# Four of a pass's seven second-layer products in quarters, in another order, with sums in every home of first-layer weights

## The chip, the core and the metric

The kernel runs on one core of one Trainium2 chip. The metric is the device time of one execution, in microseconds (us), as the median of several runs. Beside the times there is one execution taken by the hardware profiler; its trace gives every instruction with its start, length, engine, and what ended a wait before it. Engines are named as the profile names them: PE is TensorE (matmuls; PEld its weight loads), DVE is VectorE, ACT is ScalarE, POOL is GpSimd, and SP issues DMAs (transfers). SBUF is the memory beside the engines, in which tiles live; PSUM is the memory that matmuls write.

## The reference

Everything is fp32. There are 8 sequences of 512 rows and 512 columns. The reference runs four layers over them; three fifths of the time go to the part that matters here, the feed-forward network of the second layer and the expert network of the third:

```python
h = _ln(x) * g2 + beta2                                # second layer, one set of weights
ff = _gelu2(h @ W1 + b1) @ W2 + b2
x = x + ff
...
h = gelu(input @ Wi[expert] + bi[expert])              # third layer, one expert for each sequence
o = h @ Wo[expert] + bo[expert]
r = o + input; y = norm(r) * gamma[expert] + beta[expert]
```

W1 and Wi are 512x2048, W2 and Wo 2048x512. The fourth layer makes two 32-column bases orthonormal (a Gram-Schmidt process, one column after the other), and adds to every row of y a low-rank response, scaled by a gate that needs the mean of all rows of the sequence.

## The kernel before

The last stage (`mlp_stage`) makes 16 passes, q = 0 to 15, one for each sequence and network: passes 0 to 7 are the second layer, 8 to 15 the experts. A pass multiplies twice. Its **first layer** works through the 2048 hidden columns in four groups g of 512. Its **second layer** takes all four groups together.

Both layers save multiplications by a scheme with seven products in place of eight (Strassen's, in Winograd's form): each operand is cut in 2x2 quadrants, here of 256 columns, called A00 to A11 on the left and B00 to B11 on the right. Seven products are made of quadrants and of sums of quadrants (S1 to S4 on the left, T1 to T4 on the right), and added up in the right combination:

- p1 = A00 B00, p2 = A01 B10, p3 = S4 B11, p4 = A11 T4, p5 = S1 T1, p6 = S2 T2, p7 = S3 T3.

In the second layer the left operand is the activations (`acts`, [128, 4 groups, 4, 512]), the right one the tile `wo` of the same shape. `second` (L1635) makes one such product with 128x256 matmuls, into a PSUM tile y_28, y_32 and so on, by the number of its first slot. `third` (L1694) makes a product by a second level of the same scheme, in quarters of 128 columns: 7 x 4 matmuls of 128x128, 28 in place of 16 twice as wide. It accumulates into two PSUM tiles (y_48a with four quarters, y_48b with three), and DVE adds these up in a tile `yw`. In an fp32 trace each matmul is two instructions.

Before the change p7 and p4 are in quarters. The order of the second layer is p1 (slots 28 to 31), p5 (32), p2 (36), p6 (40), p3 (44), p7 (48), p4 (52). In the last pass p4 is two half products, with the end of the kernel between (`last_row`).

**Slots and hooks.** A pass has 56 slots. Slots 0 to 27 are the 28 products of the first layer (four matmuls each, seven products for each group); slots from 28 on are fourths of a second-layer product. All other work is hung on slots: `at(hooks, s, f)` puts f before the matmuls of slot s. Compute instructions are pinned (`pin`), so each engine gets them in the order in which they are written and works through them in that order. A hook's slot decides only its place in each engine's queue; when it runs is decided by what it waits for.

**Sums.** The left sums of the second layer are DVE's work. ACT first copies one operand to PSUM (`stage`, two buffers), so that DVE reads one operand from PSUM and one from SBUF. The right sums are subtractions on POOL (`gadd`, L1220). `t13` makes T1 and T3, `t2s2` T2 and S2 after each group of p5, `t4s4` T4 and S4 after each group of p2. The quarter sums are made by `quarters`: three left steps (`of_left`) and four subtractions on POOL (`of_right`), for p7 at slots 28 to 31 (right) and 40 to 42 (left), for p4 at 41 to 44 (right) and 43, 45, 47 (left).

**Homes.** The first-layer weights of one group (`wi`, 1 MB) live in one of four SBUF buffers, x0 to x3, which I call homes. Once a pass's first layer is through, homes x1 to x3 hold the quarter sums of p7 and p4; x0 is free, and takes the next pass's first group by a load at slot 21 (L2054). x1 is loaded at slot 52, x2 and x3 at slot 0 of the next pass, then `wo` (4 MB). `w_quads` makes the S sums of a loaded group on POOL: group 0 at slot 46 of the pass before (L2077), group 1 at slot 1, group 2 at slot 7, group 3 at slot 14. The first layer's third product of a group is the first that reads S2.

**What else shares the engines.** In passes 0 to 7 a Gram-Schmidt step stands at four slots (11, 25, 44, 51; L2079): `gs_norm` lets DVE reduce a broadcast row `qb` and POOL take a root (`gs_d`), and two slots later `gs_b` updates `qm` on DVE and issues the next broadcast of `qb` by two DMAs on POOL (L1259). In those passes the next sequence is also normalised. In passes 9 to 15 the tail of the sequence before runs along: `tail_gamma`, `tail_feats` (PSUM tile pf), `gate` (pg), `strength` (pz), `add_beta` (a 128x2048 addition on POOL, L1918), and four tiles `po` from slot 45, which DVE adds to the rows at slots 47, 48, 49 and 51 (`tail_add`, L1930). At slot 51 `b_quads` makes the eight right sums of the next pass's first layer on DVE, with both operands in SBUF.

**PSUM.** Products, pf, pg, pz and po take turns in six buffers, in the order in which they are written: a tile waits until the reader of the sixth tile before it is done.

Of the kernel before, what the change touches and what calls it, by code (L numbers as in the profile page):

```python
# [20 lines left out]
NB = 8  # L21
S = 512
D = 512
# [1174 lines left out]
def mlp_stage(tc, a, small, xp, io, wo8, x1d, ident, eidx, sigs, layernorm, rstd_of, phalf, wl3, g2, b1, first):  # L1198
# [4 lines left out]
    with ExitStack() as ctx:  # L1203
# [348 lines left out]
        def run(q, hooks):  # L1552
# [21 lines left out]
            def s13(g):  # L1574
# [2 lines left out]
                add(ss[g], t, act_quad(g, 1, 1))  # L1577
                add(act_quad(g, 1, 0), act_quad(g, 0, 0), t, ALU.subtract)

            for g in range(NG):  # L1580
                out = {
                    (i, j): acts[:, g, 2 * i : 2 * i + 2, H * j : H * j + H]
# [46 lines left out]
                        add(out[0, 1], p[6], u2)  # L1629
                        gelu(0)  # L1630

            wo, ts = wos[q], {}
            tvs = extra["t", q]

            def second(s, A, B, each=None):  # L1635
                y = ps.tile([P, 2, H], F32, name=f"y_{q}_{s}", tag="u", bufs=6)
                for g in range(NG):
                    go(s + g)
                    if s == 28 and g == 1:
                        stage(f"s13_{NG - 1}", act_quad(NG - 1, 1, 0))  # L1640
                    if s == 28 and g == 2:
                        s13(NG - 1)
                    for i in range(2):
                        for m in range(2):
                            mm(
                                y[:, m, :], A(g)[:, i, m * P : (m + 1) * P], B(g)[:, i, :],
                                g + i + m == 0, g + i + m == NG + 1,
                            )
                    if each:
                        each(g)  # L1650
                return y

            def quarters(key, i, j, wi_, wj, homes):


                def left(k, m):
                    o = H * i + P * m
                    return acts[:, :, 2 * j + k, o : o + P]

                def right(k, n):  # L1660
                    o = H * wj + P * n
                    return wo[:, :, 2 * wi_ + k, o : o + P]

                s1, s2, s4, t1, t2, t4 = homes
                L, M = left, right
                four[key] = dict(
                    a=((L(0, 0), M(0, 0)), (s2, t2), (L(0, 1), M(0, 1)), (s1, t1)),
                    b=((L(1, 0), M(1, 0)), (s4, M(1, 1)), (L(1, 1), t4)),
                )
                sub = ALU.subtract  # L1670
                of_left = [
                    lambda: (stage(key + "a", L(0, 1)), stage(key + "b", L(0, 0))),
                    lambda: (
                        add(s1, st[key + "a"], L(1, 1)),
                        add(L(0, 1), L(0, 0), st[key + "a"], sub),
                        stage(key + "c", L(1, 0)),
                    ),
                    lambda: (add(s2, s1, st[key + "b"], sub), add(s4, st[key + "c"], s2, sub)),
                ]
                of_right = [  # L1680
                    lambda: gadd(t1, M(0, 1), M(0, 0), sub), lambda: gadd(M(0, 1), M(1, 1), M(0, 1), sub),
                    lambda: gadd(t2, M(1, 1), t1, sub), lambda: gadd(t4, M(1, 0), t2, sub),
                ]
                return of_left, of_right

            four = {}
            homes = {}

            def quarter_homes(n):
                for k in range(1, 4)[n:]:  # L1690
                    t = xp.tile([P, KC, D], F32, name=f"q4_{q}_{k}", tag=f"x{k}", bufs=1)
                    homes[k] = [t[:, c, :].rearrange("p (g d) -> p g d", g=NG) for c in range(KC)]

            def third(s, key):  # L1694

                jobs = [
                    (n, k, g, v) for n in "ab" for k, v in enumerate(four[key][n]) for g in range(NG)
                ]
                ys = {
                    n: ps.tile([P, 4, P], F32, name=f"y_{q}_{s}{n}", tag="u", bufs=6) for n in "ab"  # L1700
                }
                w = ap.tile([P, 4, P], F32, name=f"yw_{q}_{s}", tag="tmp", bufs=4)
                y = ys["a"]
                for i, (n, k, g, (A, B)) in enumerate(jobs):
                    if i % 7 == 0:
                        go(s + i // 7)
                    last = len(four[key][n]) - 1
                    mm(
                        ys[n][:, k, :], A[:, g, :], B[:, g, :], k + g == 0,
                        k == last and g == NG - 1,  # L1710
                    )
                    if n == "a" and k == last and g == NG - 1:
                        pin(nc.scalar.copy(w[:, 0, :], y[:, 0, :]))
                        add(w[:, 1, :], y[:, 1, :], w[:, 0, :])
                        add(w[:, 2, :], y[:, 2, :], w[:, 1, :])
                        add(w[:, 1:4:2, :], y[:, 3:4, :].to_broadcast([P, 2, P]), w[:, 1:3, :])
                add(w[:, 0:3, :], ys["b"][:, 0:3, :], w[:, 0:3, :])
                return w.rearrange("p (m n) d -> p m (n d)", m=2)

            def early_quarters():  # L1720
                quarter_homes(0)
                h1, h2, h3 = (homes[k] for k in (1, 2, 3))
                return (
                    quarters("p7", 1, 0, 0, 1, (h1[3], h2[0], h2[1], h1[0], h1[1], h1[2]))
                    + quarters("p4", 1, 1, 1, 0, (h3[1], h3[2], h3[3], h2[2], h2[3], h3[0]))
                )

            def x_add(i, j, t):
                o = quad(x, i, j)
                add(o, t, o)  # L1730
# [3 lines left out]

            yu = ap.tile([P, 2, H], F32, name=f"yu_{q}", tag="yu", bufs=1)

            def t2s2(g):
                if g < NG - 1:
                    stage(f"s2_{g + 1}", act_quad(g + 1, 0, 0))
                else:  # L1740
                    stage("s4_0", act_quad(0, 0, 1))
                gadd(tvs[g], quad(wo[:, g], 1, 1), tvs[g], ALU.subtract)
                add(ss[g], ss[g], st[f"s2_{g}"], ALU.subtract)

            def t4s4(g):
                if g < NG - 1:
                    stage(f"s4_{g + 1}", act_quad(g + 1, 0, 1))
                gadd(quad(wo[:, g], 1, 0), quad(wo[:, g], 1, 0), tvs[g], ALU.subtract)
                add(act_quad(g, 0, 1), st[f"s4_{g}"], ss[g], ALU.subtract)

            l7, r7, l4, r4 = early_quarters()
            for i, f in enumerate(r7):
                at(hooks, 28 + i, f)
            for i, f in enumerate(l7):
                at(hooks, 40 + i, f)
            if q < NQ - 1:
                for i, f in enumerate(l4):
                    at(hooks, 43 + 2 * i, f)
                for i, f in enumerate(r4):
                    at(hooks, 41 + i if q <= NB else 40, f)  # L1760
            p1 = second(28, lambda g: act_quad(g, 0, 0), b(0, 0))
            pin(nc.scalar.copy(yu, p1))
            x_add(0, 0, p1)
            stage("s2_0", act_quad(0, 0, 0))
            p5 = second(32, lambda g: ss[g], lambda g: tvs[g], t2s2)
            x_add(1, 1, p5)
            x_add(0, 1, p5)
            p2 = second(36, lambda g: act_quad(g, 0, 1), b(1, 0), t4s4)
            x_add(0, 0, p2)
            p6 = second(40, lambda g: ss[g], lambda g: tvs[g])  # L1770
            add(yu, p6, yu)
            x_add(0, 1, yu)
            p3 = second(44, lambda g: act_quad(g, 0, 1), b(1, 1))
            x_add(0, 1, p3)
            p7 = third(48, "p7")
            add(yu, p7, yu)
            x_add(1, 1, yu)
            x_add(1, 0, yu)
            if q < NQ - 1:
                p4 = third(52, "p4")  # L1780
                x_add(1, 0, p4)
            else:
                for m in range(2):
                    y = ps.tile([P, H], F32, name=f"y_{q}_52_{m}", tag="u", bufs=6)
                    for g in range(NG):
                        if g % 2 == 0:
                            go(52 + 2 * m + g // 2)
                        for i in range(2):
                            mm(
                                y, act_quad(g, 1, 1)[:, i, m * P : (m + 1) * P],  # L1790
                                b(1, 0)(g)[:, i, :], g + i == 0, g + i == NG,
                            )
                    last_row(m, y)

        def t13(q, g):
            w = wos[q][:, g]
            t = io.tile([P, 2, H], F32, name=f"t_{q}_{g}", tag=f"v{g}", bufs=2)
            gadd(t, quad(w, 0, 1), quad(w, 0, 0), ALU.subtract)
            gadd(quad(w, 0, 1), quad(w, 1, 1), quad(w, 0, 1), ALU.subtract)
            extra.setdefault(("t", q), {})[g] = t  # L1800


        outs = {}
# [237 lines left out]
        for q in range(NQ):  # L2041
# [8 lines left out]
            if nx:  # L2050
                if nx >= NB:
                    at(hooks, 45, load_extra, nx)
                at(hooks, 2, load_x, nx)
                at(hooks, 21, load_wi, nx, 0)  # L2054
                at(hooks, 52, load_wi, nx, 1)
            if 1 <= q <= NB:
                at(hooks, 4, lambda q=q: nc.sync.dma_start(x2d[q - 1], xs[q - 1]))
# [6 lines left out]
            if nx:  # L2064
# [9 lines left out]
                    for c in range(KC):  # L2074
                        at(hooks, 46 + c, scale, nx, c)
                at(hooks, 51, b_quads, nx)
                at(hooks, 46, w_quads, nx, 0, gadd)  # L2077
            if q < NB:
                for i, s in enumerate((11 if q else 18, 25, 44, 51)):  # L2079
                    at(hooks, s, gs_norm, 4 * q + i)  # L2080
                    at(hooks, s + 2, gs_b, 4 * q + i)
            if q == 0:
# [119 lines left out]
```

## Time and profile before

| | |
|---|---|
| median of 3 runs | 2655.78 us (2653.2 to 2657.71) |
| the profiled execution's own time | 2656.1 us |
| its span, first to last instruction | 2654.3 us |
| granted TensorE clock | 0.995 |
| busy in the span | PE 2609.9 us (98%), DVE 1950.1 (73%), POOL 1598.1 (60%), ACT 1177.3 (44%) |
| the last stage | from 1079 us on |
| one of the passes 1 to 7 | 95.38 us (first layer 48.35, second 47.03) |
| one of the passes 9 to 14 | 98.98 us (as much, and 3.6 us of tail matmuls) |

The profile has several views. The groups give, for each line, engine and shape, the count, total and mean time, and the idle time of the engine before them. The waits tell which engine waited for whom. The chain of waits goes back from the last instruction, at each step to what released it. The timeline lists instructions in order of time. A view by stretches gives each engine's busy time between given times. `x16` is a count of instructions; names are tiles, output first (`y<-wo,act`), without buffer numbers.

### The profile page before, as it was taken

Reading aid. Unit: us, or ns where it says so; the run is one execution under the profiler, and the core shown is the slowest. Engines: PE = TensorE matmul, PEld = TensorE weight load, DVE = VectorE, ACT = ScalarE, POOL = GpSimd, SP = SyncE. Lnnn points to the kernel's source line nnn. Section 1 sums busy time; section 2 is a strip of 40 time slices with the busy share of each in tenths; the row PEclk is TensorE's granted clock in tenths of the full one; section 3 lists DMA queues with packets and bytes.
Section 4 is the critical chain, followed back from the end, with each engine's and each line's share of the span. In section 5 each row is a group of like instructions: output and inputs, shape, how many; then the busy total and the mean of one; then the engine's idle time right before and its main releaser. Section 6 shows DMA issues by size and latency. Waiting matters only on the chain.

```text
span 2654.3 us, 41760 instructions
## 1 busy us (share of the span) xinstructions
PE 2609.9 (98%) x14896; PEld 1954.8 (74%) x14896; DVE 1950.1 (73%) x3684; ACT 1177.3 (44%) x2416; POOL 1598.1 (60%) x1223
## 2 busy tenths in 40 slices
PE   6999999999999999999999999999999999999998
PEld 3455555555555555798899899898898898898897
DVE  7978798888888756577667667667567777776765
ACT  2576767776777766233233323321312422322322
POOL 3555665655555655477666766766665665666662
PEclk9999999999999999999999999999999999999999
DMA  9765756666766555552662563455245355255241
GB/s 322 253 227 187 258 195 240 215 237 207 248 227 227 170 186 170 158 165 68 167 195 53 150 196 96 127 167 166 93 147 188 98 183 195 91 187 197 86 154 41
DMA packets 241828, 460.46 MB, mean 173 GB/s; under 512 B 33904, under 2 KB 77496, under 8 KB 232534
## 3 DMA queue, kind: packets, MB, share of 16 engines
q1 hardware_dynamic: 237754, 447.04, 49.0%
q0 software_dynamic: 3552, 10.72, 4.3%
q8 instruction: 119, 1.95, 0.3%
q14 instruction: 87, 0.71, 0.1%
q10 hardware_dynamic: 316, 0.03, 0.0%
HBM read 398.43 MB, written 55.09 MB: 171 GB/s over the span
## 4 chain that ended last, share of the span: by engine, by line
PE 93%; DMA 2%; DVE 2%; ACT 1%; issue 1%; POOL 0%; SPq 0%; DVEq 0%; POOLq 0%; ACTq 0%
PE u L1211 28%; PE y L1211 21%; PE tr L564 8%; PE s L561 5%; PE ctx L561 4%; PE pv L561 4%; PE o L561 4%; PE pk L561 4%; PE pq L561 4%; PE y_48a L1211 2%; PE y_52a L1211 2%; PE y_48b L1211 2%; PE y_52b L1211 1%; PE l L253 1%; PE xb L564 1%
## 5 line engine op out<-in xcount | busy, mean ns | idle before, releaser
L998 POOL TENSOR_TENSOR bt<-bt,mk 128x1024 f32<-128x1024 f32 x256 | 542.0, 2142 | 59.3 <-DMA bt<-in_bias 49.4
L1026 ACT ACTIVATE bt<-bt,mn 128x512 f32<-128x512 f32 x512 | 365.8, 718 | 77.9 <-DVE mn L1021 77.6
L1211 PE MATMUL y<-wo,act 128*128 128x256 f32 x1568 | 352.2, 380 | 0.0
L564 PEld LDWEIGHTS tr<-ident,bt 128*128 128x128 f32 x2048 | 229.9, 142 | 150.3 <-issue 101.8
L1021 DVE CUSTOM_DVE_ANT_0 bt<-s,bt 128x512 f32<-128x512 f32 x512 | 329.9, 684 | 5.1 <-PE s L561 4.4
L1211 PE MATMUL u<-bt,wi 128*128 128x256 f32 x1440 | 330.5, 379 | 0.0
L1217 DVE TENSOR_TENSOR act<-u,u 128x512 f32<-128x512 f32 x256 | 174.1, 685 | 212.4 <-PE u L1211 155.1
L1211 PEld LDWEIGHTS y<-wo,act 128*128 128x128 f32 x1568 | 296.0, 190 | 46.2 <-issue 6.7
L1052 ACT COPY pt<-tr 128x512 f32<-128x512 f32 x376 | 207.8, 584 | 207.2 <-PE tr L564 199.8
L1211 PEld LDWEIGHTS u<-bt,wi 128*128 128x128 f32 x1440 | 272.4, 190 | 36.4
L564 PE MATMUL tr<-ident,bt 128*128 128x128 f32 x2048 | 277.0, 278 | 8.2 <-ACT pt L1052 3.5
L1211 PE MATMUL u<-tb,ws 128*128 128x256 f32 x1024 | 242.3, 379 | 1.3 <-DVE yw L1217 1.3
L1211 PE MATMUL y<-t,s 128*128 128x256 f32 x1024 | 227.8, 380 | 0.0
L1211 PEld LDWEIGHTS u<-tb,ws 128*128 128x128 f32 x1024 | 194.2, 190 | 28.2 <-issue 1.6
L1211 PEld LDWEIGHTS y<-t,s 128*128 128x128 f32 x1024 | 194.0, 190 | 26.1
L1590 ACT ACTIVATE act<-act,b 128x512 f32<-128x512 f32 x128 | 85.3, 714 | 271.9 <-DVE act L1217 207.4
L1050 DVE COPY pt<-tr 128x512 f32<-128x512 f32 x136 | 93.8, 689 | 134.0 <-PE tr L564 133.2
L1220 POOL TENSOR_TENSOR t<-wo,t 128x512 f32<-128x512 f32 x64 | 81.4, 1278 | 147.1 <-PE y L1211 147.1
L561 PE MATMUL s<-kt,qt 32*128 32x512 f32 x1024 | 165.9, 643 | 1.2 <-ACT kt L651 0.8
L1590 ACT ACTIVATE act<-act,bi 128x512 f32<-128x512 f32 x128 | 82.9, 711 | 188.1 <-DVE act L1217 188.0
L1217 DVE TENSOR_TENSOR u<-u,u 128x512 f32<-128x512 f32 x192 | 131.0, 682 | 42.7 <-PE u L1211 41.6
L1569 ACT COPY st_s<-act 128x512 f32<-128x512 f32 x192 | 111.9, 589 | 86.3 <-DVE act L1217 53.5
(378 smaller groups left out, 4852.4 us busy)
## 6 DMA issues: line engine op xcount, KB each, us to landing
bt<-in_bias SPq DMA_DIRECT2D x256, 512.0 KB
wo<-in_W SPq DMA_DIRECT2D x32, 1024.0 KB
wi<-in_Wi SPq DMA_DIRECT2D x32, 1024.0 KB
wo<-in_Wo_e SPq DMA_DIRECT2D x32, 1024.0 KB
wi<-in_W SPq DMA_DIRECT2D x28, 1024.0 KB
td<-tt SPq DMA_DIRECT2D x22, 1024.0 KB
bt<-td SPq DMA_DIRECT2D x176, 128.0 KB
gq<-coef_q SPq DMA_DIRECT2D x21, 512.0 KB
```

What stands on the lines that cost most here:

```text
L561: pin(nc.tensor.matmul(out, lhsT=lhsT, rhs=rhs, start=start, stop=stop))
L564: pin(nc.tensor.transpose(out, src, ident))
L998: nc.gpsimd.tensor_tensor(bt, bt, mask[b, r][:, None, :].to_broadcast([P, 2, S]), ALU.add)
L1021: nc.vector.tensor_tensor_reduce(bt[:, i, :], ss[h], bt[:, i, :], -1.0, 3.0e38, ALU.add, ALU.min, mn)
L1026: nc.scalar.activation(bt[:, i, :], bt[:, i, :], AF.Exp, bias=mn, scale=-1.0, accum_out=sums[b, c][:, h, r : r + 1],)
L1050: pin(nc.vector.tensor_copy(pt[:, :, r % 2, :], tr))
L1052: pin(nc.scalar.copy(pt[:, :, r % 2, :], tr))
L1211: pin(nc.tensor.matmul(out, lhsT=lhsT, rhs=rhs, start=start, stop=stop))
L1217: pin(nc.vector.tensor_tensor(out, x, y, op))
L1220: pin(nc.gpsimd.tensor_tensor(out, x, y, op))
L1569: pin(nc.scalar.copy(t, src))
L1590: nc.scalar.activation(acts[:, g, k, :], acts[:, g, k, :], func, bias=bi[:, j : j + 1])
```

## The change

In each pass p2 and p3 are made in quarters too, by `third`. The order becomes p1 (28), p5 (32), p2 (36), p6 (40), p7 (44), p3 (48), p4 (52); the last pass keeps p3 before p7.

All four homes now hold quarter sums, x2 and x3 twice in a pass (`set_up`). So the load of the next pass's first group moves from slot 21 to slot 48, behind p7, and its sums from slot 46 to slot 52. The Gram-Schmidt step of slot 44 moves to 46.

T4 and S4 go to other places: T4 to the quadrant B00 in place of B10, S4 to A00 in place of A01, since p2's quarters need A01 and B10 whole. They are made at slots 36 to 39. The staging of the last group's S1 and S3 moves one slot back, to 30 and 31.

The new functions that say where sums lie and when they are made. `r_sum` runs on POOL; `l_sum` copies on ACT and adds on DVE; in the last loop the first tuple holds the slots of `l_sum`, the second those of `r_sum`:

```python
def r_sum(key, n):
    t1, t2, t3, t4 = rt[key]
    if n == 0:
        gadd(t1, right(key, 0, 1), right(key, 0, 0), sub)
    elif n == 1:
        gadd(t3, right(key, 1, 1), right(key, 0, 1), sub)
    elif n == 2:
        gadd(t2, right(key, 1, 1), t1, sub)
    else:
        gadd(t4, right(key, 1, 0), t2, sub)

def l_sum(key, n):
    s1, s2, s3, s4 = lt[key]
    if n == 0:
        stage(key + "a", left(key, 0, 1))
        stage(key + "b", left(key, 0, 0))
    elif n == 1:
        add(s1, st[key + "a"], left(key, 1, 1))
        add(s3, left(key, 0, 0), st[key + "a"], sub)
        stage(key + "c", left(key, 1, 0))
    else:
        add(s2, s1, st[key + "b"], sub)
        add(s4, st[key + "c"], s2, sub)

def set_up(part):
    if part == 0:
        fresh(2)
        r_homes("p2", *hx[2])
    elif part == 1:
        fresh(0, 1, 3)
        l_homes("p2", *hx[3])
        r_homes("p7", *hx[0][0:3])
        r_homes("p3", *hx[1][0:3])
    elif part == 2:
        fresh(2, 3)
        l_homes("p7", hx[0][3], hx[1][3], hx[2][0])
        r_homes("p4", *hx[2][1:4])
        l_homes("p3" if last else "p4", *hx[3][0:3])
    elif not last:
        l_homes("p3", *(
            io.tile([P, NG, P], F32, name=f"s4_{q}_{i}", tag=f"v{i}", bufs=2)
            for i in range(3)
        ))

tail, last = q > NB, q == NQ - 1
four = (40, 41, 42), (44, 45, 46)
for part, s in enumerate((25, 28, 40, 44)):
    at(hooks, s, set_up, part)
for key, ss_, ts_ in (
    ("p2", (28, 29, 30), (25, 26, 27, 28)),
    ("p7", four[last], (29, 30, 31, 31)),
    ("p3", four[not last], (40, 40, 40, 40) if tail else (40, 41, 42, 43)),
    ("p4", (47, 48, 49), (44, 44, 44, 44) if tail else (43, 44, 45, 46)),
):
    ...
```

The rest of the diff, cut to its core:

```diff
-                gadd(quad(wo[:, g], 1, 0), quad(wo[:, g], 1, 0), tvs[g], ALU.subtract)
-                add(act_quad(g, 0, 1), st[f"s4_{g}"], ss[g], ALU.subtract)
+                gadd(quad(wo[:, g], 0, 0), quad(wo[:, g], 1, 0), ts[q, g], ALU.subtract)
+                add(act_quad(g, 0, 0), st[f"s4_{g}"], ss[g], ALU.subtract)
...
-            p2 = second(36, lambda g: act_quad(g, 0, 1), b(1, 0), t4s4)
+            p2 = third(36, "p2")
             x_add(0, 0, p2)
...
-            p3 = second(44, lambda g: act_quad(g, 0, 1), b(1, 1))
-            x_add(0, 1, p3)
-            p7 = third(48, "p7")
-            add(yu, p7, yu)
-            x_add(1, 1, yu)
-            x_add(1, 0, yu)
+            for s, key in zip((44, 48), ("p3", "p7") if last else ("p7", "p3")):
+                p = third(s, key)
+                if key == "p3":
+                    x_add(0, 1, p)
+                else:
+                    add(yu, p, yu)
+                    x_add(1, 1, yu)
+                    x_add(1, 0, yu)
...
-                at(hooks, 21, load_wi, nx, 0)
+                at(hooks, 48, load_wi, nx, 0)
                 at(hooks, 52, load_wi, nx, 1)
...
-                at(hooks, 46, w_quads, nx, 0, gadd)
+                at(hooks, 52, w_quads, nx, 0, gadd)
...
-                for i, s in enumerate((11 if q else 18, 25, 44, 51)):
+                for i, s in enumerate((11 if q else 18, 25, 46, 51)):
```

## The prediction

> **What bounds the kernel now.** I read four views: the groups of instructions, the waits of PE, the chain of one pass, and the timelines of DVE and POOL where passes meet. Everything that the change touches lies in the last stage, 16 passes from 1079 us on.
>
> The waits of PE over that stage (1075 to 2654 us), complete but for three waits at the kernel's very end (columns: total us, times, longest):
>
> ```profile
> PE u L1211 <- DVE yw L1217: 1.3, 1, 1.3
> ...
> PE pg L1211 <- DVE qd L1292: 0.3, 1, 0.3
> ```
>
> The chain of work from 1360 to 1470 us, the fifth pass (start, length, matmuls):
>
> ```profile
> 1365.78 48.35 PE u L1211 x224
> 1414.13 34.53 PE y L1211 x160
> 1448.66 3.57 PE y_48a L1211 x32
> 1452.23 2.68 PE y_48b L1211 x24
> 1454.91 3.57 PE y_52a L1211 x32
> 1458.49 2.68 PE y_52b L1211 x24
> ```
>
> So TensorE is the bound, without a gap: a pass is 95.38 us and is nothing but matmuls. In fp32 a matmul counts as two instructions. A whole product of the second layer is 32 of them, 34.53/5 = 6.91 us (216 ns each); one in quarters is 56, 3.57 + 2.68 = 6.25 us (112 ns each).
>
> What the other engines have left, by stretches (length, then busy PE, PEld, DVE, ACT, POOL): second layer of the fifth pass, then that of a late pass (2189 to 2240 us):
>
> ```profile
> 1414.13:1448.66 34.53, 34.53 (x162) 30.40 (x162) 25.72 (x47) 16.20 (x27) 25.71 (x23) 1.00 0.30 65
> 1448.66:1461.17 12.51, 12.51 (x114) 12.51 (x113) 9.32 (x22) 0.99 (x3) 4.84 (x5) 1.00 0.63 118
> ...
> 2189.04:2227.16 38.12, 38.12 (x212) 32.47 (x212) 27.88 (x36) 15.87 (x29) 24.13 (x16) 1.00 0.33 97
> 2227.16:2239.67 12.51, 12.51 (x114) 12.51 (x113) 9.94 (x23) 0.53 (x2) 2.63 (x3) 1.00 0.74 254
> ```
>
> DVE is busy 35.0 of 47.0 us here and 37.8 of 50.6 there. That is the slack that the change spends.
>
> **What it takes off.** Two more products per pass in quarters: 2 x (6.91 - 6.25) = 1.31 us of PE. All 16 passes have both p2 and p3 (the last lacks only p4, as before), so 16 x 1.31 = **21.0 us**, if nothing waits.
>
> The trace shows the price of a 128-column matmul directly, 112 ns against 216 ns for 256 columns, 52%. The Trainium skill, "TensorE: Matmul & The Clock Gate", section "Back-to-back issue gap", speaks against small matmuls: it gives some 81 ns at 128 columns and 131 ns at 512 for a stream with weight loads; a straight line between them (an estimate from that page) makes 128 columns 83% of 256, so a quartered product some 1.45 times a whole one, 3.1 us dearer, and 32 of them 99 us slower. The rows decide for 52%.
>
> **What it adds.** Per product, DVE gets four sums at a 0.60 us pitch (2.4), three small adds of the accumulators (1.0) and one of 384 columns (0.55): 4.0 us; two products, 8.0. The add into x, which read PSUM (0.68), now reads SBUF, at 0.69 us with POOL idle but 1.36 on average in the rows of x<-yw,x: 1.3 more per pass. DVE goes to 43 to 44 of 45.7 us, and to 46 to 47 of 49.3 in late passes. POOL gets eight subtractions of 1.28 us (10.2 us), and ACT six copies of 0.59 and two of 0.27: 4.1 us; ACT has 17 of 47 us busy, so that is hidden.
>
> Sums of p2 and p7 on POOL: I count POOL forward in the fifth pass. The sums of p2 and p7 end near 59 us of the pass (before, those of p7 alone ended at 57.8), t2 near 64, t4 near 69, p3's at 75, p4's at 82; their users start at 62, 68, 88, 82 and 88 us. Hidden, by 3 us at the least. t4 no longer waits for PE, since it writes B00, which p1 has finished with. p2's left sums end near 55.4 and s13 of the last group near 56.8, 2 us later than before; p5 needs the latter at 60.4. Hidden. p7's left sums end at 73.2 (needed 76.2), p3's at 81.7 (s2 needed 82.5), p4's s2 at 88.3 (needed 88.7). Hidden by less and less.
>
> **What comes out late in the passes 1 to 8: S2 of the first group.** The load of home 0 moves from slot 21 to 48, behind p7, where it waits for PE. Behind it on SP stand only the stores of earlier rows and the load of home 1, which is bound to PE anyway. The load takes some 5.4 us (issue 2233.45, first sum 2238.84), so home 0 is there 5 us before the pass ends. But its sums on POOL moved from slot 46 to 52, and so past a Gram-Schmidt step: POOL now first does gs_d, which waits for DVE's norm, which waits for the qb broadcast, which POOL issues only when DVE has finished qm. These are the rows of that chain, from the timelines of POOL and DVE:
>
> ```profile
> 1451.50 1.06 POOL L1259 DMA_DIRECT2D qb<-qm  x2
> 1458.84 0.95 POOL L1243 TENSOR_TENSOR gs_d<-gn_s,phalf 64x1 f32<-64x1 f32 x1 [6.28 <-DVE gn_s L1236]
> ...
> 1458.06 0.68 DVE L1236 CUSTOM_DVE_ANT_0 junk_gn<-qb 64x512 f32<-64x512 f32 x1 [1.43 <-DMA qb<-qm]
> ```
>
> In the changed order p7 ends at 75.32 + 6.25 = 81.57 us of the pass. DVE's evacuation of it (2.5 us, 1459.29 to 1461.81) and gs_b (1.5) come next; DVE gets there some 0.9 us late, since p3's sums and the first accumulator of p7 lie before: qm at 86.5. Then 1.05 (issue) + 5.5 (landing, 1452.56 to 1458.06) + 0.78 + 1.0 (gs_d) + 1.35 (S1) + 1.6 (S2, as in the row beside a busy DVE) = 11.3: S2 at 97.8. PE wants it at the third product of the next pass, 94.07 + 3.45 = 97.5. Bounds: with DVE on time 96.9, no wait; in the last two passes the landing took 6.9 us, which makes 1.7. Five of seven landings were at 5.5, so I take a wait of **0.5 us**, eight times: 4.0. Pass 0 has a longer queue on POOL (add_row at slot 26, 4.5 us) and 3 us more on DVE: 1 us, between 0 and 3.
>
> **What comes out late in the passes 9 to 15.** Two operands in SBUF make DVE wait for POOL:
>
> ```profile
> 2219.87 4.13 DVE L1217 TENSOR_TENSOR x<-yu,x 128x512 f32<-128x512 f32 x1
> ...
> 2218.95 4.51 POOL L1220 TENSOR_TENSOR x<-x,beta 128x2048 f32<-128x2048 f32 x1
> ```
>
> The 0.69 us add ended 0.5 us after POOL's 4.5 us one. In the changed order the same pair stands in front of p3's sums and of the accumulators of p7: POOL's add from 77.2 to 81.7, x at 82.3, p3's four sums 84.7, the three adds that free y_44a 85.8. p3 is due at 85.2 (p2 with pf and pg ends at 70.5, p6 at 77.6, then 6.25 + 1.3 for po). Six PSUM buffers go round, and y_44a, y_44b and four po fill them, so y_48a needs the one that y_44a held. Wait **0.7 us** (0 to 1.5), seven times: 4.9. In the same way the next pass's second product needs po_3's buffer: DVE reads po_3 after b_quads, whose two-operand sums now meet POOL's sums of home 0. Alone it would be done at 99.3, after four waits of 1.28 at 102.6, and it is due at 100.1: I take 0.2 (0 to 2.5), six times: 1.2. At the kernel's end the last p3 is evacuated by two adds instead of one before the norm: 0.6, once.
>
> The Trainium skill, "SBUF — State Buffer", section "Who interferes with whom", has the rule behind these rows, and it speaks against the change: a DVE instruction with two SBUF inputs blocks for a whole GpSimd instruction that reads SBUF. By the rule each of the two added SBUF adds would cost up to 1.28 us, 2.6 a pass, all in the stretch where DVE is nearly full.
>
> **Sum**, against the profiled execution (2656.1 us, span 2654.3; the median of the runs is 2655.8): 2656.1 - 21.0 + 4.0 + 1.0 + 4.9 + 1.2 + 0.6 = **2647 us**. A difference under 0.2% (5.3 us) can't be told from none here.
>
> **The rivals.**
> 1. All is hidden: 2656 - 21 = 2635. For it: PE waits nowhere now, and the due times above are missed by under 1 us. Against it: two of them are missed.
> 2. The gain is eaten: the landing is 6.3 us (1.3 a pass, eight times) and po_3 is 0.6 late; 10.4 + 1 + 4.9 + 3.6 + 0.6 = 20.5, so 2655.6. For it: the load of home 1 is now issued with qb, and home 0 is still landing.
> 3. Slower, by one mechanism: S2 behind gs_d. With the 6.9 us landing and DVE 1 us later than I count, S2 is 2.7 us late in eight passes, 21.6 in place of 4.0: 2665. It turns to a loss in these passes from 1.31 us on, at a landing of 6.3 with my DVE. For it: DVE at 95% of that stretch. Against it: DVE has idle time in the first layer (31 of 48 us) to catch up, so lateness doesn't add up over passes.
> 4. The change doesn't do what it says: excluded, for the changed kernel's PE order has y_36a, y_36b, y_44a and y_44b in every pass.
>
> **Chances.** Forecast 0.34 (2642 to 2650), all hidden 0.16, eaten 0.25, slower 0.25. Faster by over 0.2% is the first two, 0.50; within 0.25; slower 0.25. The likeliest case lies in 2642 to 2650; the range takes in the others, up to S2 3 us late: 2635 to 2667.
>
> **What would show it.** Each pass before 8 should be 94.1 us plus a wait of u for POOL ws; y_36 and y_44 should read 3.57 + 2.68. In late passes PE should wait for DVE yw at y_48a, and for DVE x (L1980) at the second u. If no such waits appear, rival 1 holds; if the wait for ws is over 1.3 us, rival 3. I would be wrong altogether if PE waits inside the second layer, at p7 or p4, for DVE's left sums.

## The result, and the profile after

The changed kernel takes 2694.87 us (median of 4 runs, 2693.42 to 2696.76), the kernel before 2654.49 (4 runs beside it): a ratio of 1.0155, 95% interval 1.0136 to 1.0173. It is 40 us **slower**; the forecast was 2647, the range 2635 to 2667. The profiled execution took 2695.44 us. Its last stage is 45.5 us longer than before; the stage ahead of it, which the change does not touch, happened to be 6 us shorter.

The seven largest waits of PE in the last stage of the changed kernel (total us, times, longest), to be held against the two waits shown of before:

```profile
PE u L1211 <- DVE x L1980: 23.5, 5, 7.2
PE u L1211 <- POOL ws L1220: 6.5, 7, 1.8
PE u L1211 <- DVE u L1217: 2.8, 2, 1.9
PE u L1211 <- DVE yw L1217: 2.8, 1, 2.8
PE y L1211 <- ACT act L1701: 2.6, 1, 2.6
PE y_48a L1211 <- DVE yw L1217: 2.5, 6, 0.4
PE y_44a L1211 <- DVE q L1217: 2.1, 1, 2.1
```

The expected waits are there (ws at the start of passes 2 to 8, y_48a in late passes), at about the expected size. The first line is the one that was priced at 1.2 us: a product at the start of a pass waits for DVE's addition of po_3 (`tail_add`, now L1980). It is the third product, not the second as the prediction has it, so the buffer of po_3 goes to the seventh tile after it and not to the sixth. Laid out by the starts of the passes in PE's timeline, the 45.5 us are, in us against before:

| where | change |
|---|---|
| the quarters themselves, 16 x 1.31 | -21.0 |
| pass 0: second layer 54.18, not 45.84 | +8.3 |
| first layers of passes 1 to 8 | +8.9 |
| second layers of passes 1 to 6, 46.02 and not 45.73 | +1.8 |
| second layers of passes 9 to 14, 49.97 and not 49.32 | +3.9 |
| **first layers of passes 9 to 15** (49.6 to 58.8, not 48.35) | **+42.2** |
| second layer of pass 15 and the kernel's end | +1.4 |

The place where pass 10 meets pass 11, from DVE's timeline in the changed kernel (start, length, what; x2 are two instructions):

```profile
2143.18 1.39 DVE L1217 TENSOR_TENSOR tb<-bt 128x256 f32<-128x256 f32 x1
...
2151.55 6.11 DVE L1217 TENSOR_TENSOR tb<-bt,tb 128x256 f32<-128x256 f32 x2
2157.58 0.74 DVE L1980 SCALAR_TENSOR_TENSOR x<-po,st,x 128x512 f32<-128x512 f32 x1
```

POOL's timeline beside it:

```profile
2141.67 1.27 POOL L1220 TENSOR_TENSOR ws<-wi 128x512 f32<-128x512 f32 x1 [5.17 <-DMA wi<-in_Wi]
...
2145.67 1.44 POOL L1220 TENSOR_TENSOR ws<-wi,ws 128x512 f32<-128x512 f32 x1
2147.07 1.45 POOL L1220 TENSOR_TENSOR ws<-wi 128x512 f32<-128x512 f32 x1
...
2152.71 4.67 POOL L1220 TENSOR_TENSOR x<-x,bo_e 128x2048 f32<-128x2048 f32 x1
```

PE's timeline at the same place (in brackets the pause; a product is eight instructions):

```profile
2147.75 3.62 PE L1211 MATMUL u<-bt,wi 128*128 128x256 f32 x16
2158.47 3.75 PE L1211 MATMUL u<-tb,ws 128*128 128x256 f32 x8 [7.10 <-DVE x L1980]
```

And before, POOL (the last sum of home 0, the first of home 1):

```profile
2227.68 1.28 POOL L1220 TENSOR_TENSOR ws<-wi,ws 128x512 f32<-128x512 f32 x1
2238.84 1.27 POOL L1220 TENSOR_TENSOR ws<-wi 128x512 f32<-128x512 f32 x1 [9.88 <-DMA wi<-in_Wi]
```

DVE beside it, before (the first and the last of the eight sums `tb` and `bt`, 3.0 us in all):

```profile
2232.06 0.42 DVE L1217 TENSOR_TENSOR tb<-bt 128x256 f32<-128x256 f32 x1
...
2234.32 0.75 DVE L1217 TENSOR_TENSOR tb<-bt,tb 128x256 f32<-128x256 f32 x2
```

In the changed kernel, from 2141.67 to 2157.4, POOL works without a gap: four sums of home 0, four of home 1, the long addition to x. DVE's sums have both operands in SBUF; each waits for one of POOL's, the last for the addition. Eight sums take 14.5 us, po_3 is read by 2158.3, and PE, which wanted its buffer at 2151.4, starts at 2158.47.

The other late passes say the same in other sizes. The eight sums took 9.16, 10.99, 11.16, 14.48 and 14.57 us, and the waits for x behind them were 1.78, 3.61, 3.78, 7.10 and 7.20: each time 7.4 us less. Ahead of pass 15, where the sums took 6.61 us, there was no wait for x.

The same stretch by windows (window, length, then busy PE, PEld, DVE, ACT, POOL; granted clock, DMA share, GB/s):

```profile
2147.75:2152.00 4.25, 3.62 (x18) 2.85 (x16) 4.25 (x4) 0.59 (x1) 4.17 (x4) 1.00 0.00 0
2152.00:2158.50 6.50, 0.03 (x1) 0.06 (x1) 6.50 (x4) 0.00 (x0) 5.37 (x2) 0.61 0.00 0
2158.50:2165.00 6.50, 6.50 (x19) 5.30 (x20) 4.59 (x10) 0.00 (x0) 0.00 (x0) 0.60 0.90 302
```

PE stands still for 7.1 us; in the 6.5 us after that it is busy throughout, but at a clock of 0.60. The loss is the wait and then some: of the 42.2 us, 29.1 are waits (23.5, 2.8 and 2.8 above), 13.1 the slower matmuls after them.

In pass 0, DVE's timeline:

```profile
1122.30 5.01 DVE L1276 TENSOR_TENSOR al<-al,below 64x1 f32<-64x1 f32 x1
```

and POOL's:

```profile
1121.56 4.52 POOL L1220 TENSOR_TENSOR x<-x,b2row 128x2048 f32<-128x2048 f32 x1
```

A sum of one column took 5.01 us, since POOL's addition, which now has one of p2's sums ahead of it, had just begun. (Before, the same two met as well, but halfway through the addition: 2.56 us.) PE waited 2.6 us for an activation behind it, and later 2.1 for p7's left sums.

### The profile page after: what moved, and what is told of

It is laid out like the page before. It is cut to its first block, busy times and chain, and to the rows that moved or that the text cites. A ratio compares the mean times of both kernels' runs of the same rounds, so it can differ in the third digit from the quotient of the medians.

```text
span 2693.7 us, 43813 instructions
## 1 busy us (share of the span) xinstructions
PE 2604.5 (97%) x15664; PEld 1968.6 (73%) x15664; DVE 2172.3 (81%) x3940; ACT 1231.5 (46%) x2544; POOL 1783.0 (66%) x1351
## 5 line engine op out<-in xcount | busy, mean ns | idle before, releaser
L998 POOL TENSOR_TENSOR bt<-bt,mk 128x1024 f32<-128x1024 f32 x256 | 541.7, 2140 | 58.8 <-DMA bt<-in_bias 49.9
L1211 PE MATMUL u<-tb,ws 128*128 128x256 f32 x1024 | 250.5, 389 | 32.8 <-DVE x L1980 23.5
L1220 POOL TENSOR_TENSOR q<-wo,q 128x512 f32<-128x512 f32 x126 | 170.7, 1355 | 4.4
L1220 POOL TENSOR_TENSOR wo<-wo 128x512 f32<-128x512 f32 x111 | 142.1, 1281 | 8.7
```

Source lines behind the costliest of these rows:

```text
L998: nc.gpsimd.tensor_tensor(bt, bt, mask[b, r][:, None, :].to_broadcast([P, 2, S]), ALU.add)
L1211: pin(nc.tensor.matmul(out, lhsT=lhsT, rhs=rhs, start=start, stop=stop))
L1220: pin(nc.gpsimd.tensor_tensor(out, x, y, op))
```

## The experiments

All times are medians, with the ratio to the kernel before run beside each. The theory at the start: b_quads beside POOL's unbroken run of work, here called the train, makes po_3 late; PE waits, and then runs at a lower clock.

**1. b_quads on POOL in late passes**

```diff
-                at(hooks, 51, b_quads, nx)
+                at(hooks, 51, b_quads, nx, False, gadd if q > NB else add)
```

> The changed kernel, but in passes 8 to 14 POOL and not DVE makes the eight right sums of the next first layer (b_quads). POOL stands idle there for 5.2 to 6.3 us, before home 0 has landed; eight sums at half the 1.28 us of a 128x512 one are an estimated 5.2 us. Theory (DVE's two-operand sums take turns with POOL's sums of homes 0 and 1 and its addition to x, po_3's buffer comes late, PE waits 26 us in all and then runs at a lower clock for another 16 us): the waits of PE for x at the second u go, and with them the low clock; 2694.9 - 42 = 2653, 2648 to 2658. Rival A (home 0 itself comes too late, since its load moved): POOL has 5.2 us more ahead of home 0's sums, so no gain, 2690 to 2700, and PE waits for ws. Rival B (DVE is simply full with the new quarter sums): DVE is relieved of 3.0 us a pass, at most 6 x 3 = 18 us come back, 2677.

2658.44 us, ratio 1.0025 (1.0015 to 1.0036). The first layers of passes 9 to 15 are back at 48.35, and of the waits above, the first, third and fourth line are gone. DVE still makes all quarter sums, so it was not too full for them in these passes. Home 0 still comes as late (its load is issued 13.2 us before pass 10 ends, 13.0 in the changed kernel), so it was not that. This is the largest part of the loss, undone by one move. (By `q > NB` it starts with pass 9; in pass 8 the sums stay on DVE.) Of the 5 us above my number the trace shows some 3.7: second layers of passes 9 to 14 of 50.22 in place of 49.97, and passes 0 and 8, each about 1 us longer than in the changed kernel.

**2. po_3 ahead of b_quads**

```diff
-                    at(hooks, (47, 48, 49, 51)[r], tail_add, o, r)
+                    at(hooks, (47, 48, 49, 50)[r], tail_add, o, r)
```

> The changed kernel, with the last row's addition of po_3 one place earlier in DVE's queue, ahead of b_quads and not behind it. If what is late is only po_3's buffer, as the prediction priced it, the waits of PE for x and the low clock behind them go: 2694.9 - 42 = 2653. If it is the stretched b_quads, everything behind it stays late: y_48b's evacuation moves up by only the 0.7 us of po_3's addition, its buffer is that of the fourth u, which PE would take 3.6 us after the second one: waits of 7.1 become 3.4, those of 3.7 vanish, about half of the 42 us comes back: 2674, 2665 to 2682, and the waits are for yw.

2686.72 us, 1.0113 (1.0088 to 1.0138). The four runs lie far apart, from 2677.18 to 2698.68, and the trace is of the longest. In it the waits for x are gone, but six for yw (15.7 us) and three for u (6.0) stand in their place, in pass 11 one of 5.66. Even less came back than I expected: whatever stands behind the stretched sums is late, and the buffer of po_3 was only the first to be missed.

**3. The long addition to x later**

```diff
-            at(hooks, 2 if q else 26, add_row, q)
+            at(hooks, 15 if q > NB else 2 if q else 26, add_row, q)
```

> The changed kernel, with POOL's 128x2048 addition to x in passes 9 to 15 from slot 2 to slot 15, away from b_quads' end. Theory: the alternation with the sums of homes 0 and 1 stays (10.9 us for eight sums that take 3.0 alone), only the last sum's 4.7 us behind the long addition goes, in the passes where it was caught (11 and 12, waits of 7.1 and 7.2 become 3.6), and the add to x behind it elsewhere: 8 us of waits and some 5 of low clock come back, 2682, 2675 to 2688. Rival C (the long addition alone is the cause): all 42 come back, 2653. Rival D (POOL's work has no part in it): unchanged, 2695.

2678.92 us, 1.0092 (1.0075 to 1.0109). The waits for x fall from 23.5 to 14.9 us, the longest from 7.2 to 3.8: the addition is a part of the train, the smaller one.

**4. and 5. Only a delay, in the kernel before**

```diff
+            for _ in range(24 if r == 3 else 0):    # 13 in the second run
+                pin(nc.vector.tensor_scalar(x[:, r, :], x[:, r, :], 1.0, None, ALU.mult))
             pin(nc.vector.scalar_tensor_tensor(x[:, r, :], t["po", r], ...
```

> The kernel before, with a single delay: in passes 9 to 15 DVE multiplies the last row of x by one, in place, 24 times, ahead of the addition of po_3. By a row of 0.54 us for such an instruction 24 are 13.0 us; po_3 was read 7.3 us before PE wanted its buffer, so PE should wait about 5.7 us in each of passes 10 to 15, 34 us in all. No sum, load or place of the change is in it. Theory (a wait of a few us is followed by a lower granted clock, which costs 0.6 us for each us of wait, 16 to 26 as in the changed kernel): 2654.5 + 34 + 20 = 2709, with a granted clock of 0.6 to 0.8 in the 6 us after each wait. Rival E (the low clock in the changed kernel came from its many narrow matmuls, or from the load of all engines): 2654.5 + 34 = 2688, at a clock of 1.0 after the waits.

2742.16 us, 1.0333 (1.0316 to 1.035). An instruction took 0.79 us, not 0.54, so the waits were 10.1 us and not 5.7: 60.6 in six passes. First layers of passes 10 to 15 grew by 76.5, so 2.65 us for each pause came on top (two more waits of 0.5 us are in that), far from the 0.6 us for each us of wait that I had read out of the changed kernel. Another 11.7 us lie in the second layer of pass 15 and the kernel's end, with a wait of 8.7 us. The windows around one pause (matmuls from 2154.50 on, the pause from 2156.4 to 2166.5):

```profile
2154.50:2164.00 9.50, 1.89 (x9) 1.33 (x7) 9.22 (x9) 0.00 (x0) 6.60 (x3) 0.80 0.44 165
2164.00:2168.00 4.00, 1.53 (x4) 1.29 (x5) 3.79 (x8) 0.00 (x0) 0.00 (x0) 0.50 0.21 79
2168.00:2172.00 4.00, 4.00 (x15) 3.31 (x14) 3.79 (x9) 0.00 (x0) 0.00 (x0) 0.70 0.95 294
2172.00:2176.00 4.00, 4.00 (x20) 3.53 (x19) 3.76 (x7) 0.00 (x0) 0.00 (x0) 1.00 1.05 398
```

Nothing of the change is in this kernel, so the low clock belongs to the pause. It lasts some 4 us after the pause ends (5 in the changed kernel, after 7.1 us).

> The kernel before with 13 in place of 24 multiplications ahead of po_3's addition. 24 took 19.0 us and made waits of 10.1 us, so 13 take 10.3 us, and the six waits should be 1.4 us each, 8.3 in all. In the run with 24 a pass was longer by 2.5 to 3.1 us than its wait, in the changed kernel by 2.5 to 3.3 us too, with waits of 3.6 to 7.2. If each pause costs that, whatever its length: 2652.3 + 8.3 + 6 x 2.7 = 2677. If the cost grows with the wait as between nothing and 10.1 us (0.27 us for each us): 2652.3 + 8.3 + 2.2 = 2663.

2706.56 us, 1.0185 (1.0157 to 1.0213): both expectations missed. The multiplications did end earlier, but DVE's next addition with two operands in SBUF then met POOL's long one (3.64 us for 0.69), and a pass had up to three pauses, fifteen in six passes, 32.3 us in all. Their first layers grew by 45.3, 13.0 more than the waits, less for each pause than with 10.1 us. A delay of DVE can't be made shorter here without meeting something else.

**6. Half of the change: p2 alone in quarters**

```diff
-                p = third(s, key)
+                p = second(s, lambda g: act_quad(g, 0, 0), b(1, 1)) if key == "p3" else third(s, key)
...
-                at(hooks, 48, load_wi, nx, 0)
+                at(hooks, 21, load_wi, nx, 0)
...
-                at(hooks, 52, w_quads, nx, 0, gadd)
+                at(hooks, 46, w_quads, nx, 0, gadd)
```

and no sum in home 0.

> Half of the change: p2 in quarters in all passes, p3 whole. Its nine sums fit in homes 1 to 3, so home 0 is free again, is loaded at slot 21 and summed at slot 46 as in the kernel before; order, T4 and S4 as in the changed kernel. PE saves 16 x 0.655 = 10.5 us. Theory (the loss comes from home 0's sums, which run beside b_quads and start a train of POOL work, and in pass 0 from the place of the addition to x): no waits for x, yw or ws where passes meet, pass 0 keeps its 8 us if DVE's al again meets the addition; 2652.3 - 10.5 + 0 to 8 = 2642 to 2650, with a few us for y_48a. Rival B (DVE full): p2's sums alone are half of the added 9 us a pass, half of the loss stays, 2665 or more.

2671.56 us, 1.0059 (1.0043 to 1.0076): my theory's number failed, and so did the theory as I had worded it, with home 0's sums as the start of the train. The number lies in Rival B's range, but the trace speaks against a DVE that is full: its sums wait here too, the fourth one 4.63 us beside POOL's addition. POOL, where pass 10 meets pass 11 (DVE's b_quads ran from 2135.56 to 2145.70):

```profile
2132.84 1.27 POOL L1220 TENSOR_TENSOR ws<-wi,ws 128x512 f32<-128x512 f32 x1
2134.07 1.26 POOL L1220 TENSOR_TENSOR ws<-wi 128x512 f32<-128x512 f32 x1
...
2139.46 4.69 POOL L1220 TENSOR_TENSOR x<-x,bo_e 128x2048 f32<-128x2048 f32 x1
```

Home 0 is early again; but p7, whose right sums are in home 1, now comes before p3, so home 1 is loaded some 7 us earlier in the pass (2126.97, 37.0 us into the second layer; 44.6 in the kernel before, 43.9 in the changed one), and its sums and the addition follow home 0's without a gap. The train reached b_quads from the other end. Six pauses of 2.5 to 2.7 us came of it.

**7. The Gram-Schmidt step behind the sums of home 0**

```diff
-                for i, s in enumerate((11 if q else 18, 25, 46, 51)):
+                for i, s in enumerate((11 if q else 18, 25, 46, 54)):
                     at(hooks, s, gs_norm, 4 * q + i)
-                    at(hooks, s + 2, gs_b, 4 * q + i)
+                    at(hooks, min(s + 2, 55), gs_b, 4 * q + i)
```

> The changed kernel, with the Gram-Schmidt step of slots 51 and 53 in passes 0 to 7 at 54 and 55, behind the sums of home 0 on POOL. The prediction held that S2 is late because these sums stand behind the step: the seven waits for ws, 6.5 us, go, and 2694.9 - 6.5 - 2 = 2686. Theory (b_quads beside the sums of home 0 is what costs): in passes 1 to 8 the step was what kept the two apart; now b_quads takes turns there too, up to 8 us longer, and the waits for ws become waits for yw or for the next sums, with the low clock behind them: 2694.9 plus 0 to 40, so not faster than 2690.

2685.72 us, 1.0115 (1.0096 to 1.0134): the number that the prediction's step gives. All seven waits for ws are gone, first layers of passes 1 to 7 are back at 48.35. My theory of that moment failed here: b_quads does meet home 0's four sums now (5.2 us for eight), but nothing follows them on POOL, which waits for DVE again, and 2 us more on DVE are hidden. So four sums are harmless; the train is what costs.

**8. and 9. Home 1's sums taken out of the train**

```diff
-                at(hooks, 52, load_wi, nx, 1)
+                if q <= NB:
+                    at(hooks, 52, load_wi, nx, 1)
...
             if q:
+                if q > NB + 1:
+                    at(hooks, 0, load_wi, q, 1)
```

> The changed kernel, with one load moved: in passes 9 to 14 home 1 is loaded at slot 0 of the next pass, behind the store of the last rows, and not at slot 52. b_quads stays on DVE and home 0's sums stay where the change put them, but home 1's sums and the long addition to x come later than b_quads. In passes 1 to 7 of the run with the later Gram-Schmidt step b_quads met four of POOL's sums and nothing behind them: 5.2 us for eight sums that take 3.0 alone. Theory as it now stands (what makes po_3 late is the train of POOL's sums of two homes and the addition, 10.9 to 14 us): b_quads ends 6 us earlier, po_3 is read 2 us before PE wants its buffer, the waits for x and the low clock go: 2694.9 - 42 = 2653, 2650 to 2665. Rival A (home 0's own sums, which the change moved, are what meets b_quads): waits of 1 to 3 us stay in five passes, with the clock 20 us: 2675.

2688.36 us, 1.0125 (1.0108 to 1.0142). The trace shows the load of home 1 issued at 2142.16, still ahead of the store of the last rows (2153.27) and, as before, 6.06 us before the pass ends: transfers that are not pinned go out on SP in another order than that of their slots. (The "one us later" of the next expectation is not in these rows: home 1 was issued 6.06 us before the pass ended in both kernels.) The case was not made. With load and store pinned on SP:

> The same intent as the run with home 1's load at slot 0, in which the load still went out ahead of the store, one us later than before: now the load and the stores of the rows are pinned on SP, so the load of home 1 in passes 9 to 14 stands behind the store that waits for po_3's addition. b_quads (DVE, from 2143 in the eleventh pass) then meets four of POOL's sums at most, those of home 0. Theory (the train behind them is the cause): eight sums in 5 to 6 us, po_3 read some 2 us before PE wants its buffer, no waits for x; home 1 lands 6.5 us after 2150, its sums end at 2162, S2 of the second group at 2159.5, wanted at 2163; 2694.9 - 42 = 2653, 2650 to 2660. Rival A (the four sums of home 0, which the change moved, are enough): waits for x stay in the late passes, 2670 or more.

2665.89 us, 1.0044 (1.003 to 1.0057). DVE at the same place:

```profile
2138.17 1.27 DVE L1217 TENSOR_TENSOR tb<-bt 128x256 f32<-128x256 f32 x1
...
2142.30 0.42 DVE L1217 TENSOR_TENSOR tb<-bt,tb 128x256 f32<-128x256 f32 x1
...
2143.98 0.74 DVE L1982 SCALAR_TENSOR_TENSOR x<-po,st,x 128x512 f32<-128x512 f32 x1
```

Eight sums in 5.9 us, po_3 read by 2144.7, 1.5 us before PE wants its buffer; home 1's sums begin at 2151.34. All waits for x are gone, with b_quads on DVE and home 0's sums where the change put them, so Rival A falls. 34 of the 42 us are back. What is left of them are four waits for u (4.8 us). Ahead of the longest, 2.26 us in pass 15, POOL's addition, which now runs later, meets a small DVE instruction of the next norm (3.66 us for 0.17); the first, 0.91 in pass 9, was there in the changed kernel too; for the other two no cause is shown. That is 8 of the 13 us by which the run lies above my number; the other 5 I can't place.

**10. to 12. The mended kernel**

```diff
-                at(hooks, 51, b_quads, nx)
+                at(hooks, 51, b_quads, nx, False, gadd)
...
-            at(hooks, 2 if q else 26, add_row, q)
+            at(hooks, 2 if q else 18, add_row, q)
...
             add(yu, p6, yu)
-            x_add(0, 1, yu)
+            if tail:
+                at(hooks, 47, x_add, 0, 1, yu)
+            else:
+                x_add(0, 1, yu)
```

and the Gram-Schmidt step as in the seventh experiment.

> The changed kernel with four other places: b_quads on POOL in all passes; the addition to x of pass 0 at slot 18 and not 26; the Gram-Schmidt step of slots 51 and 53 at 54 and 55; in passes 9 to 15 the add of yu to x behind p3's left sums, so that it no longer stands in front of y_44a's adds beside POOL's long addition. From the run with POOL's b_quads in the late passes (2658.4): pass 0 gives 8 us, the waits for ws 7, y_48a 0.9 in seven passes, 6: 2637, 2632 to 2646. All of the 21 us that the quarters save on PE would then show but some 4. Against it: in passes 0 to 7 POOL is fuller, and if its eight sums push home 0's S2 beyond PE's third product, the waits for ws stay: 2650 or more.

2644.99 us, 0.997 (0.9952 to 0.9988), 8 above my number: pass 0 gave 6 of its 8 us, and of the waits for ws two of 0.2 us were left, but moving the add of yu only moved y_48a's wait to y_52a (3.3 us in passes 9 to 14, and 0.6 in pass 0), since p4's left sums then came later. In the next kernel b_quads moves to POOL in late passes alone, the add of yu stays where the change had it, and the addition of beta is cut:

```diff
+            for r in range(R):
+                gadd(x[:, r, :], x[:, r, :], beta)
-            gadd(x, x, beta[:, None, :].to_broadcast([P, R, D]))
```

> The changed kernel with b_quads on POOL in passes 8 to 14 alone, the addition to x of pass 0 at slot 18, the Gram-Schmidt step at 54 and 55, and POOL's long addition of beta to x cut into four of one row each, so that DVE's add of yu waits for at most one of them. Against the first mended kernel (2645.0): b_quads back on DVE in passes 0 to 7 takes off the small waits for ws, 0.3 us in each of 7 passes, and 1.6 in pass 8; y_48a should be free in time, 0.4 of wait and as much behind it in 6 passes: 2645 - 2 - 1.6 - 3 = 2638, 2634 to 2644. If the four short additions only spread the same meeting over more of DVE's adds, 2641 to 2646.

2640.41 us, 0.9947 (0.993 to 0.9963): y_48a's wait is gone, y_52a's is 2.5 us in all (0.6 of it in pass 0). On top of it:

```diff
-                    at(hooks, (47, 48, 49, 51)[r], tail_add, o, r)
+                    at(hooks, (47, 50, 50, 51)[r], tail_add, o, r)
```

> The second mended kernel with the additions of po_1 and po_2 from slots 48 and 49 to 50, behind p4's left sums on DVE. PE waited there for the last of these sums (y_52a for q, 0.3 to 0.6 us, 2.5 in 7 passes, with some 0.1 of slower matmuls each); two additions of 0.67 us less stand ahead: these waits go, 2640.4 - 3 = 2637. If the sums wait for ACT's copies or for PE and not for DVE, nothing changes: 2640.

2634.79 us, **0.9926 (0.9912 to 0.994)**: 20 us faster than the kernel before. All waits of PE in its last stage:

```profile
PE y_44a L1211 <- DVE q L1217: 1.3, 1, 1.3
PE y_52a L1211 <- DVE q L1217: 0.6, 1, 0.6
PE ytr L1214 <- DVE x L1878: 0.4, 1, 0.4
PE ytr L1214 <- DVE x L2010: 0.4, 1, 0.4
PE pz L1211 <- ACT h L2054: 0.4, 1, 0.4
```

Late passes are 97.67 us, 1.31 less than before: the whole of the quarters' gain. It has the change's products, homes and load places; only five places in queues differ (b_quads, on POOL in late passes, the first addition to x, one Gram-Schmidt step, two additions of po) and one addition is cut in four.

## Why the prediction was wrong

Step by step:

- **The quarters, -21.0: right.** A late pass of the last kernel is 1.31 us shorter, as 32 x (6.91 - 6.25) over 16 says.
- **S2 behind gs_d, 0.5 each, 4.0 (bounds 0 to 13.6): right in mechanism, low in size.** Seven of the eight waits came, 0.5 to 1.8 us long; the first layers grew by 8.9 us. The seventh experiment moved that step, its waits went, and the kernel was 9.2 us faster.
- **Pass 0, 1 (0 to 3): mis-sized, 8.3.** I counted POOL's longer queue and DVE's work, and did not ask which DVE instruction the shifted addition would meet.
- **y_48a, 0.7 each, seven times, 4.9: right in kind, a little high.** Six waits of 0.4, 3.9 us with what came behind. **The kernel's end, 0.6:** 1.4.
- **po_3, the step that failed**: "Alone it would be done at 99.3, after four waits of 1.28 at 102.6, and it is due at 100.1: I take 0.2 (0 to 2.5), six times: 1.2." It cost 42.2. The due time was too early (PE wants the buffer one product later, and the runs leave 7.4 us for the eight sums), so four sums alone cost nothing, as the ninth experiment shows; what failed is how much of POOL's work the eight sums meet. I let b_quads meet the four sums of home 0 and stopped there. The rows of before showed what comes next: POOL ended home 0's sums at 2228.96 and began home 1's at 2238.84, and b_quads, 2232.06 to 2235.0, lay in the gap. Moving home 0's sums 9 us back (they began 34.5 us into the second layer, now 43.9) closes the gap: home 1 has landed when home 0's four sums are done, 5.4 us after they began, and the long addition (4.67 us) follows. A sum of DVE that is held back by one of these four meets the next four. The first, third and ninth experiment show it: without the train (by another engine, or a later load) the waits for x go; with its last part gone they fall to 14.9.
- **No term for what follows a pause.** Before, PE paused only twice ahead of the kernel's end, for 1.3 and 0.3 us, so no row had a price for a pause of some us; the bounds should have named it as unknown. 13 of the 42 us are that.
- **p4's left sums**, counted as ready 0.4 us ahead of time, were 0.3 us late in six passes (1.8 us).

Of the rivals, the third was on the right side for a wrong reason: its place cost 8.9 us, not 21.6. Without the 42.2 us of po_3 the time would be 2653, inside the range. "All is hidden: 2656 - 21 = 2635" is what the last kernel reached, after five more moves in the queues and a cut. The sign I called "wrong altogether", waits for left sums inside the second layer, appeared once (pass 0, 2.1 us): DVE's load, which I watched most closely, was not where it broke.

The prediction quoted the Trainium skill, "SBUF — State Buffer", section "Who interferes with whom", for the two added adds alone. The traces agree with it: DVE's sums wait for whole instructions of POOL, up to 5.01 us for one column. They show one thing more: where both engines have a queue they take turns, and POOL is slowed too (1.27 to 1.45 us for a sum).

Of the clock, "TensorE: Matmul & The Clock Gate", section "What's actually happening", says that the clock is halved after an idle window of some 3.4 us, and full again after a busy one. The runs agree in kind (0.5 in the window at the end of a 10 us pause, full some 4 us after it). But the six pauses of the sixth experiment, 2.5 to 2.7 us, are shorter than a window, and two of them were followed by matmuls at half speed.

What stays open: how the 13.0 us of the fifth experiment divide among its pauses, and whether p4's left sums could come in time in passes 1 to 6, where they cost 0.3 us even in the last kernel. In the changed kernel's pass 3 DVE is busy from 1447.86 until the sum that PE waits for ends, at 1454.94, and the update of the Gram-Schmidt step (1451.56 to 1453.15) stands ahead of it; no run moves that update.

## What to carry to other kernels

When an instruction moves in a queue, look at the gap that it leaves and at the gap that it fills: the cost here was not the meeting of two groups of work but that a third one lay just behind. For each DVE instruction with two operands in SBUF near the end of a stage, ask what POOL has from there on until it next waits, and count that whole stretch. And where the bound engine has hardly paused, give a pause a price of its own: the wait, and here up to some 3 us behind it.

## What the runs showed of the hardware

Six pauses of PE of nearly the same length, in the kernel with p2 alone in quarters. Its PE timeline, the eight matmul instructions after three of them (start, length; in brackets the pause):

```profile
2146.59 1.97 PE L1211 MATMUL u<-tb,ws 128*128 128x256 f32 x8 [2.54 <-DVE x L1974]
...
2248.20 3.65 PE L1211 MATMUL u<-tb,ws 128*128 128x256 f32 x8 [2.56 <-DVE x L1974]
...
2453.18 3.62 PE L1211 MATMUL u<-tb,ws 128*128 128x256 f32 x8 [2.55 <-DVE x L1974]
```

Four were followed by matmuls at full speed, two by matmuls at half. The first layers were 51.1 to 51.3 us long in the one case, 52.8 in the other, against 48.35 without a pause. In the kernels run here, of the pauses ahead of eight such instructions of 256 columns none up to 1.8 us was followed by slow ones, every one from 2.85 us on was, and in between it went either way. The price of a pause above its own length was 0.2 to 0.4 us without the low clock and 1.8 to 3.3 with it, about as much after 3.6 us as after 10.
